# Pair attention: the softmax sum's reciprocal goes through memory and is applied to the aggregate; the weights are multiplied and stored in halves

## The chip, the cores and the metric

The kernel runs on one core of a Trainium2 chip. A time is the device time of one execution in microseconds. The kernel before took 7536.76 us, the median of three runs (7522.86 to 7555.75). The profile is of one further execution, recorded by the hardware profiler.

The core has five instruction streams that matter here[...]: TensorE (PE in the profile), VectorE (DVE), ScalarE (ACT), GpSimd (POOL) and SyncE (SP). They wait for each other by semaphores. SP and ACT also issue the DMA transfers of this stage. A DMA issue is an instruction in its engine's stream[...].

## The reference, cut to what matters

The program is a chain of eight layers on an activation `x` of shape (4, 64, 64, 128): deformable convolution, expert choice, triangle, recurrent, Fourier, mixture of experts, pair attention, mixture of experts. The change touches pair attention alone. For each of the four batch elements, with 64 rows, 64 columns, four heads and 32 channels per head, it computes:

```
p = (einsum('bxyi,ie->bxye', x, W) + b).reshape(B, N, N, HEADS, HD)
pn = layernorm(p, ln_g, ln_b)
scores = einsum('bxahd,bayhd->bxayh', pn, pn) / sqrt(HD)
att = softmax(scores, axis=2)
x_upd = layernorm(einsum('bxahd,bayhd->bxayhd', p, p), ln_g, ln_b)
agg = einsum('bxayh,bxayhd->bxyhd', att, x_upd).reshape(B, N, N, EMBED)
out = concatenate([x, agg], -1) @ Wf + bf
return layernorm(out, ln2_g, ln2_b)
```

The softmax runs over `a`. Its denominator, called z here, depends on head, x and y alone, and so does not depend on the index over which the aggregate sums. Dividing every weight by z before the sum over `a`, and dividing the finished sum by z, give the same result.

## The kernel before, in words

The four batch elements are computed one after another (the loop `for b in range(4)` at the end of `stage_pair_attention`). Each goes through three phases. The instructions of each engine are put in order when the program is built, by a list scheduler that uses its own estimates of time; the order in the source is not always the order that an engine runs.

**project** normalises x, projects it to p, and writes two copies to memory: `xd` (the normalised x, transposed) and `pd` (p by position). It keeps p, its squares and its normalised form in SBUF as `pT`, `p2` and `pn`.

**weights** computes for each head `rs`, the reciprocal standard deviation of the products p times p, and then the softmax. The heads go in two pairs, `hp` = 0 and 1, and i = 0 and 1 is the head within the pair. A tile `s[i]` of one head has 128 partitions (two values of `a`, times the 64 of x) and 2048 columns (two more values of `a`, the group index g from 0 to 15, and 64 columns y). `a` is 4 g plus two bits. The steps for one pair are:

- 128 small matmuls (line 2387) write the scores to PSUM tiles `po`; ACT copies them to `s` (L2413) and DVE keeps a running maximum (L2415).
- DVE reduces the maximum (L2420), PE swaps the two partition halves by a matmul (L2422), and DVE takes the larger (L2423).
- For each i, DVE subtracts the maximum (L2425) and ACT takes the exponential (L2426).
- For each i, four matmuls (L2430) sum the exponentials over partition halves and part of the columns into a PSUM tile `pz`. DVE then multiplies `s[i]` by `rs` in place (L2431), reduces `pz` to z (L2432), takes the reciprocal (L2433), and multiplies `s[i]` by it in place (L2434).
- Two DMAs per head (L2436), both on SP, write `s[i]` to the memory tensor `wd`, one for each half of the partitions. `wd` has the order head, a bits, x, g, y. Each contiguous piece is 1024 values, 4 KB.

The in-place product at L2431 overwrites what the matmuls of L2430 read, so that it can't start until the four matmuls of its head are done.

**combine** sums over `a`. The 64 rows x are done in eight blocks of 8 (`xg`), and each block has 64 units: 16 groups g times four heads. A unit is one matmul with 32 rows (`spread`, L2484), `S` from a tile `L` (p, loaded from `pd`) and a tile `R` (the weights, loaded from `wd`). DVE multiplies S by `q4` into `t` (L2496), for three or four units at once, and a second matmul per unit (`gather`, L2512) sums `t` into the PSUM accumulator `acc`. There are two S tiles, of four and three units, each with one buffer. `load_right` (L2461) fills one R for half of the groups of a block: `load_right(0)` reads g = 0 to 7 of the first block, `load_right(1)` reads g = 8 to 15. Each is eight DMAs, four on SP and four on ACT, and R is used only when all eight have landed. The first two loads are issued at the start of combine, and wait for the stores to `wd`.

At the end of each block `project_out` copies the accumulator from PSUM to `agg` (L2518, on ACT), does eight matmuls with the output weights (L2523 and L2524, into `pof`, which takes the one buffer that `acc` had), copies the result (L2526, ACT), adds the bias (L2527, POOL), and normalises it: statistics on DVE (L2531, L2532), a square root on ACT (L2534), a reciprocal and a small product on DVE (L2535, L2537), and scale and shift on ACT (L2539) and POOL. The tile `lx` (L2511), a load of `xd` on SP into the two buffers of the tag `xT`, is the other half of the concatenation.

Below, a "block end" is this passage from one accumulator to the next, with its 8 matmuls on PE.

Of the kernel before, what the change touches and what calls it, by code (L numbers as in the profile page):

```python
# [10 lines left out]
F32 = mybir.dt.float32  # L11
I32 = mybir.dt.int32
AF = mybir.ActivationFunctionType
ALU = mybir.AluOpType
AX = mybir.AxisListType
# [2201 lines left out]
def stage_pair_attention(k, w, bvec, ln_g, ln_b, wf, bf, ln2_g, ln2_b, blk32):  # L2217
# [14 lines left out]

    nc, tc = k.nc, k.tc
    with ExitStack() as octx:
        wp = octx.enter_context(tc.tile_pool(name="pa_w", bufs=1))
        dr = octx.enter_context(tc.tile_pool(name="pa_d", bufs=2, space=DRAM))
# [28 lines left out]
        both = wp.tile([128, 128], F32, tag="both", name="both")  # L2267
# [20 lines left out]
        sm = octx.enter_context(tc.tile_pool(name="pa_s", bufs=2))  # L2288
# [80 lines left out]
                nc.gpsimd.tensor_scalar(pn[:, c8, :], pn[:, c8, :], vec[:, 2:3], None, op0=ALU.add)  # L2369
            return pT, pn, p2  # L2370

        def weights(ps, wd, pT, pn, p2):
            rs = [big.tile([128, 2, 16, 64], F32, tag="rs", name="rs", bufs=4) for _ in range(4)]
            turn = [0]

            def products(hp, src):

                for a1 in range(2):
                    for half in range(2):
                        po = [ps.tile([128, 8, 64], F32, tag=t, name="po") for t in (("h0", "h1"), ("A", "B"))[turn[0] % 2]]  # L2380
                        turn[0] += 1
                        for j in range(8):
                            for i in range(2):
                                hr = slice(64 * hp + 32 * i, 64 * hp + 32 * i + 32)
                                for a2 in range(2):
                                    a = 4 * (8 * half + j) + 2 * a2 + a1
                                    nc.tensor.matmul(  # L2387
                                        po[i][64 * a2 : 64 * a2 + 64, j, :], src[hr, :, a], src[hr, a, :], start=True, stop=True
                                    )
                        at = (slice(None), a1, slice(8 * half, 8 * half + 8))  # L2390
                        for i in range(2):
                            yield i, at, po[i]

            for hp in range(2):
                for i, at, po in products(hp, pT):
                    nc.scalar.activation(rs[2 * hp + i][at], po, AF.Square, scale=1.0 / 32.0)
                for i, at, po in products(hp, p2):
                    t = rs[2 * hp + i][at]
                    nc.vector.tensor_tensor(t, po, t, op=ALU.subtract)
                    nc.gpsimd.tensor_scalar(t, t, 0.0, None, op0=ALU.max)  # L2400
            for r in rs:
                nc.scalar.activation(r, r, AF.Ln, bias=k.eps5)
            for r in rs:
                nc.scalar.activation(r, r, AF.Exp, scale=-0.5)
            R = [sixteen("X0", [8, 8, 64], "R0")]
            nc.gpsimd.memset(R[0], 0.0)
            for hp in range(2):
                pair = sixteen(("X3", "X2")[hp], [2, 2, 16, 64], "s")
                s = [pair[:, i] for i in range(2)]
                run = [sm.tile([128, 512], F32, tag="sq", name="run") for _ in range(2)]  # L2410
                wide = lambda t: t.rearrange("p (v y) -> p v y", y=64)
                for n, (i, at, po) in enumerate(products(hp, pn)):
                    nc.scalar.copy(s[i][at], po)  # L2413
                    if n >= 2:
                        nc.vector.tensor_tensor(wide(run[i]), po, wide(run[i]) if n >= 4 else s[i][:, 0, 0:8], op=ALU.max)  # L2415
                flat = lambda t: t.rearrange("p u v y -> p (u v) y")
                mx = sm.tile([128, 2, 64], F32, tag="mx", name="mx")
                z = sm.tile([128, 2, 64], F32, tag="z", name="z")
                for i in range(2):
                    nc.vector.tensor_reduce(mx[:, i, :], run[i].rearrange("p (v y) -> p y v", y=64), axis=AX.X, op=ALU.max)  # L2420
                    pm = ps.tile([128, 64], F32, tag="AB"[i], name="pmx")
                    nc.tensor.matmul(pm, swap, mx[:, i, :], start=True, stop=True)  # L2422
                    nc.vector.tensor_tensor(mx[:, i, :], mx[:, i, :], pm, op=ALU.max)  # L2423
                for i in range(2):
                    nc.vector.tensor_tensor(flat(s[i]), flat(s[i]), mx[:, i : i + 1, :].to_broadcast([128, 32, 64]), op=ALU.subtract)  # L2425
                    nc.scalar.activation(s[i], s[i], AF.Exp, scale=1.0 / math.sqrt(32.0))  # L2426
                for i in range(2):
                    pz = ps.tile([128, 8, 64], F32, tag=f"h{i}", name="pz")
                    for n in range(4):
                        nc.tensor.matmul(pz, both, flat(s[i])[:, 8 * n : 8 * n + 8, :], start=(n == 0), stop=(n == 3))  # L2430
                    nc.vector.tensor_tensor(s[i], s[i], rs[2 * hp + i], op=ALU.mult)  # L2431
                    nc.vector.tensor_reduce(z[:, i, :], pz.rearrange("p v y -> p y v"), axis=AX.X, op=ALU.add)  # L2432
                    nc.vector.reciprocal(z[:, i, :], z[:, i, :])  # L2433
                    nc.vector.tensor_tensor(flat(s[i]), flat(s[i]), z[:, i : i + 1, :].to_broadcast([128, 32, 64]), op=ALU.mult)  # L2434
                    for a2 in range(2):
                        nc.sync.dma_start(  # L2436
                            wd[2 * hp + i, 2 * a2 : 2 * a2 + 2].rearrange("a x g y -> x a (g y)"),
                            s[i][64 * a2 : 64 * a2 + 64].rearrange("p u v y -> p u (v y)"),
                        )
            R.append(sixteen("X1", [8, 8, 64], "R1"))  # L2440
            nc.gpsimd.memset(R[1], 0.0)
            return R

        def load_left(n, pd):
            xg, half = divmod(n, 2)
            for h in range(4):
                for a4 in range(4):
                    r = 32 * h + 8 * a4
                    (nc.sync, nc.scalar)[a4 % 2].dma_start(
                        Ls[n % 2][r : r + 8, :, 32 * a4 : 32 * a4 + 32],  # L2450
                        bass.AP(pd.tensor, pd.offset + (512 * xg + 32 * half + a4) * 128 + 32 * h, [[8192, 8], [512, 8], [1, 32]]),
                    )

        def combine(b, xd, pd, wd, Rs):
            with tc.tile_pool(name="pa_cp", bufs=1, space=PSUM) as ps:

                def load_right(n):
# [9 lines left out]
                groups, u = [], 0  # L2467
                while u < 512:
                    c = min((4, 3)[len(groups) % 2], 512 - u)
                    groups.append((u, c))  # L2470
                    u += c
                acc, out, lxs = {}, {}, {}

                def spread(i):
                    u0, c = groups[i]
# [26 lines left out]
                def gather(i):  # L2502
                    u0, c = groups[i]
                    t = out.pop(i)
                    for j in range(c):
                        xg, u = divmod(u0 + j, 64)
                        h = u % 4
                        if u == 0:
                            acc[0] = ps.tile([128, 512], F32, tag="acc", name="acc")
                            lx = lxs[xg] = sm.tile([128, 512], F32, tag="xT", name="lx")  # L2510
                            nc.sync.dma_start(lx, xd[:, 512 * xg : 512 * xg + 512])  # L2511
                        nc.tensor.matmul(acc[0][32 * h : 32 * h + 32, :], sum4, t[:, j, :], start=(u < 4), stop=(u >= 60))  # L2512
                        if u == 63:
                            project_out(xg)

                def project_out(xg):
                    agg = sm.tile([128, 512], F32, tag="sq", name="agg")
                    nc.scalar.copy(agg, acc[0])  # L2518
                    lx = lxs.pop(xg)
                    po = ps.tile([128, 4, 128], F32, tag="acc", name="pof")  # L2520
                    for j in range(4):
# [26 lines left out]
                for i in range(len(groups) + 2):  # L2548
                    if i < len(groups):
                        spread(i)  # L2550
                    if i >= 2:
                        gather(i - 2)

        ready = stats(0)
        for b in range(4):
            xd = dr.tile([128, 4096], F32, tag="xd", name="xd")
            pd = dr.tile([4096, 128], F32, tag="pd", name="pd")
            wd = dr.tile([4, 4, 64, 16, 64], F32, tag="wd", name="wd")
            with tc.tile_pool(name="pa_ps", bufs=2, space=PSUM) as ps:
                p = project(b, ps, xd, pd, *ready)  # L2560
                load_left(0, pd)
                load_left(1, pd)
                Rs = weights(ps, wd, *p)
            if b < 3:
                ready = stats(b + 1)
            combine(b, xd, pd, wd, Rs)


def prep_conv3(w):
# [57 lines left out]
```

## Time and profile before

| what | value |
|---|---|
| median of three runs | 7536.76 us |
| the profiled execution | 7520.84 us, its span 7519.0 us |
| TensorE / VectorE / ScalarE / GpSimd busy | 86% / 64% / 38% / 20% of the span |
| mean granted TensorE clock | 0.9 |
| pair attention in the trace | from about 5106 us to about 7176 us |
| combine, first S matmul to the last accumulator's copy, batch element 0 | 5283.21 to 5623.97 us |
| the same, elements 1, 2, 3 | 5798.47 to 6138.85, 6310.73 to 6650.49, 6822.56 to 7163.61 us |

Times are read from the start of the span. A row of a group gives line, engine, operation, output and inputs, the shape, and the number of instructions; after the first bar the busy time in us and the mean of one in ns; after the second the idle time of the engine before these instructions and what ended most of it. A row of the timeline has start, length, engine, line, operation, and in brackets the idle time before it with what ended it. "x8" on PE counts the records of the profile, of which a matmul on f32 has two. The chain of work is followed back from the end of a stretch, at each step to what released it. A row of the windows view has the busy time of PE, its weight loads, DVE, ACT and POOL, then the granted clock, the busy share of the 16 DMA engines, and the GB/s that they moved.

### The profile page before, as it was taken

The numbers are of one execution on the slowest core, as the hardware profiler recorded it, in microseconds if no ns is written. First come the engines' busy times: TensorE is split into PE (matmuls) and PEld (weight loads), VectorE is DVE, ScalarE is ACT, GpSimd is POOL, SyncE is SP. The second block draws the span as 40 slices with busy tenths as digits, with TensorE's granted clock in tenths as the row PEclk, the third lists the DMA queues.
The fourth block names the chain that finished last, engine by engine and source line by source line (L and its number), as shares of the span: only waits on it lengthen the run. The fifth ranks groups of instructions, "written<-read, shape, count | busy, mean of one in ns | idle before, by whom it ended". The sixth has DMA issues, their size and how long they took to land. (4 is left out here: it accounts for less than half of the span.)

```text
span 7519.0 us, 156903 instructions
## 1 busy us (share of the span) xinstructions
PE 6475.0 (86%) x63791; PEld 3490.8 (46%) x63791; DVE 4812.9 (64%) x10774; ACT 2842.8 (38%) x6717; POOL 1518.8 (20%) x1218
## 2 busy tenths in 40 slices
PE   7996888866688789799989988798897997998989
PEld 3443666654455553255555555445224234252244
DVE  2113877754577437588756566674885876857877
ACT  3332555543243326411156665564013022040055
POOL 0001222210011100055522221253012111120135
PEclk9997888987889899899989899797997997988989
DMA  4436788871300130300000000001111111111101
GB/s 120 98 89 195 210 246 242 244 227 60 137 1 2 34 67 9 116 23 23 25 10 9 9 10 4 9 1 42 34 25 50 26 39 34 27 32 41 23 23 31
DMA packets 673783, 498.10 MB, mean 66 GB/s; under 512 B 296822, under 2 KB 588600, under 8 KB 669208
## 3 DMA queue, kind: packets, MB, share of 16 engines
q1 hardware_dynamic: 510158, 399.80, 18.9%
q10 hardware_dynamic: 162890, 88.11, 4.4%
q8 instruction: 509, 8.34, 0.5%
q14 instruction: 226, 1.85, 0.1%
HBM read 335.28 MB, written 152.33 MB: 65 GB/s over the span
## 5 line engine op out<-in xcount | busy, mean ns | idle before, releaser
L2496 DVE TENSOR_TENSOR t<-S,q 128x1536 f32<-128x1536 f32 (+3 forms) x608 | 1157.0, 1949 | 120.7 <-PE S L2484 115.5
L2484 PE MATMUL S<-R,L 32*128 32x512 f32 x4096 | 734.6, 651 | 90.1 <-DMA R<-wd 78.6
L2512 PE MATMUL acc<-t,sum 128*32 128x512 f32 x4096 | 639.6, 608 | 0.0
L2198 PE MATMUL pe<-ew,yT 128*128 128x512 f32 x1024 | 480.6, 604 | 25.2 <-DVE xs L2204 22.3
L1797 PE MATMUL acc<-w,attT 128*64 128x264 f32 x4096 | 485.2, 390 | 11.0 <-DVE w L1793 11.0
L2484 PEld LDWEIGHTS S<-R,L 32*128 32x128 f32 x4096 | 200.4, 186 | 611.2 <-issue 280.1
L2518 ACT COPY agg<-acc 128x512 f32<-128x512 f32 x32 | 18.8, 586 | 1192.6 <-DMA L<-pd 855.4
L792 DVE COPY_PREDICATED band<-bit,band 128x384 f32<-128x384 int32 (+11 forms) x384 | 312.5, 929 | 186.4 <-ACT band L783 149.8
L773 PE MATMUL S<-kpad,qm 32*64 32x192 f32 (+3 forms) x8192 | 365.8, 405 | 72.4 <-ACT band L783 37.7
L2204 DVE SCALAR_TENSOR_TENSOR xs<-pe,gate,xs 128x128 f32<-128x128 f32 x1024 | 333.1, 346 | 96.9 <-PE pe L2198 80.3
L1790 POOL TENSOR_TENSOR w<-xtl,ei 128x528 f32<-128x528 f32 x256 | 332.1, 1319 | 310.5 <-ACT ei L1789 202.5
L1793 DVE TENSOR_TENSOR w<-xtl,pe 128x1056 f32<-128x1056 f32 x256 | 320.4, 1251 | 99.5 <-ACT ei L1789 88.6
L1797 PEld LDWEIGHTS acc<-w,attT 128*64 128x64 f32 x4096 | 283.5, 137 | 197.1 <-DVE w L1794 38.3
L2207 ACT ACTIVATE sc<-pe,gate 128x128 f32<-128x128 f32 x1024 | 291.2, 375 | 199.5 <-PE pe L2198 192.4
L773 PEld LDWEIGHTS S<-kpad,qm 32*64 32x64 f32 x8192 | 265.6, 151 | 128.8 <-issue 65.3
L514 PE MATMUL dw<-pad,diag 32*32 32x512 f32 x6912 | 307.4, 612 | 13.2 <-issue 7.3
L884 PE MATMUL pt<-ident,D 128*128 128x128 f32 x1536 | 259.8, 319 | 66.3 <-DMA D<-dd 48.4
L2512 PEld LDWEIGHTS acc<-t,sum 128*32 128x32 f32 x4096 | 92.7, 108 | 458.4 <-issue 436.1
L2198 PEld LDWEIGHTS pe<-ew,yT 128*128 128x128 f32 x1024 | 185.6, 193 | 232.1 <-issue 151.5
L2527 POOL TENSOR_TENSOR o<-o,bf 128x512 f32<-128x512 f32 x32 | 40.7, 1271 | 1228.5 <-ACT o L2526 1228.5
L886 ACT COPY dt<-pt 128x512 f32<-128x512 f32 x384 | 205.5, 595 | 146.2 <-PE pt L884 145.7
L884 PEld LDWEIGHTS pt<-ident,D 128*128 128x128 f32 x1536 | 214.6, 203 | 87.6 <-DMA D<-dd 52.3
(520 smaller groups left out, 12716.7 us busy)
## 6 DMA issues: line engine op xcount, KB each, us to landing
vb<-vd SPq DMA_DIRECT2D x272, 256.0 KB
D<-dd SPq DMA_DIRECT2D x128, 192.0 KB
D<-dd SPq DMA_DIRECT2D x128, 168.0 KB
D<-dd SPq DMA_DIRECT2D x128, 144.0 KB
w<-in_e_weight_dram ACTq DMA_DIRECT2D x16, 1024.0 KB
w<-in_e_weight_dram SPq DMA_DIRECT2D x16, 1024.0 KB
wd<-s SPq DMA_DIRECT2D x32, 512.0 KB
D<-dd SPq DMA_DIRECT2D x128, 120.0 KB
```

Of the source, the lines that this page charges most:

```text
L514: nc.tensor.matmul(acc[g][32 * c : 32 * c + 32], diag[r, j, tap, :], pads[j][r, y0 : y0 + 8, tx : tx + 64], start=(tap == 0), stop=(tap == 8),
L773: ins = nc.tensor.matmul(acc[g][64 * h : 64 * h + 64].rearrange("p (a s) c -> p a s c", a=3), qm[rows, h, m, :], keys, start=(m == 0), sto ...
L792: nc.vector.copy_predicated(flat[:, :, 0:n], bit[:, 0, :, i : i + 1].to_broadcast([128, 48, n]), flat[:, :, s : s + n])
L884: ins = nc.tensor.transpose(pt[:, g, :], D[:, g, ty : ty + 382 : 3], k.ident)
L1790: nc.gpsimd.tensor_tensor(w2[:, 2:4], xt[:, 2:4, 0:2], window(ei, 0, [[0, 2], [0, 2], [1, 132]]), op=ALU.mult)
L1793: nc.vector.tensor_tensor(w1, xt[:, :, 1:3], window(pe, 0, [[0, 4], [0, 2], [1, 132]]), op=ALU.mult)
L1797: nc.tensor.matmul(acc[b // 2][64 * (b % 2) : 64 * (b % 2) + 64], attT[:, b // 2, hp, 64 * (b % 2) : 64 * (b % 2) + 64], src[:, b].rearran ...
L2198: nc.tensor.matmul(pe[h].rearrange("p e c -> p (e c)"), yT[:, 128 * t : 128 * t + 128], ew[:, 4 * h : 4 * h + 4, :].rearrange("p e c -> p ...
L2204: nc.vector.scalar_tensor_tensor(xt, pe[0][:, e, :], gate[:, t, e : e + 1], xt, op0=ALU.mult, op1=ALU.add)
L2484: nc.tensor.matmul(S[:, j, :], Ls[n % 2][r, ag, :], Rs[n % 2][r, ag].rearrange("p x y -> p (x y)"), start=True, stop=True)
L2496: nc.vector.tensor_tensor(t[:, j0:j1].rearrange("p u (x y) -> p u x y", x=8), S[:, j0:j1].rearrange("p u (x y) -> p u x y", x=8), qf[:, q0 ...
L2512: nc.tensor.matmul(acc[0][32 * h : 32 * h + 32, :], sum4, t[:, j, :], start=(u < 4), stop=(u >= 60))
```

## The change

1. In `weights`, the product of the weights with 1/z (L2434) is dropped. z and its reciprocal are still computed, and for each head a [64, 64] tile is written to a new memory tensor `zd` by a DMA on SP: four per batch element.
2. Both heads' matmuls for z now stand before both heads' products with `rs`. The product of one head is split by g into two halves of 1024 columns. After each half, its two stores go out, one on SP and one on ACT: 16 stores of 256 KB per batch element instead of eight of 512 KB on SP alone. The contiguous pieces are 512 values, 2 KB.
3. In `combine`, `agg` is no longer copied by ACT: DVE multiplies the accumulator in PSUM by `zx`, a tile that a DMA on SP loads from `zd` for each block, every row of a head repeated for its 32 channels. `zx` takes a buffer of the tag `xT`, so that `lx` and `zx` of one block now hold both.

```diff
-        def weights(ps, wd, pT, pn, p2):
+        def weights(ps, wd, zd, pT, pn, p2):
...
+                pzs = []
                 for i in range(2):
-                    pz = ps.tile([128, 8, 64], F32, tag=f"h{i}", name="pz")
+                    pzs.append(ps.tile([128, 8, 64], F32, tag=f"h{i}", name="pz"))
                     for n in range(4):
-                        nc.tensor.matmul(pz, both, flat(s[i])[:, 8 * n : 8 * n + 8, :], start=(n == 0), stop=(n == 3))
-                    nc.vector.tensor_tensor(s[i], s[i], rs[2 * hp + i], op=ALU.mult)
-                    nc.vector.tensor_reduce(z[:, i, :], pz.rearrange("p v y -> p y v"), axis=AX.X, op=ALU.add)
+                        nc.tensor.matmul(pzs[i], both, flat(s[i])[:, 8 * n : 8 * n + 8, :], start=(n == 0), stop=(n == 3))
+
+                for g in range(2):
+                    c8 = slice(8 * g, 8 * g + 8)
+                    for i in range(2):
+                        nc.vector.tensor_tensor(s[i][:, :, c8], s[i][:, :, c8], rs[2 * hp + i][:, :, c8], op=ALU.mult)
+                        for a2 in range(2):
+                            (nc.sync, nc.scalar)[a2].dma_start(
+                                wd[2 * hp + i, 2 * a2 : 2 * a2 + 2, :, c8].rearrange("a x g y -> x a (g y)"),
+                                s[i][64 * a2 : 64 * a2 + 64, :, c8].rearrange("p u v y -> p u (v y)"),
+                            )
+                for i in range(2):
+                    nc.vector.tensor_reduce(z[:, i, :], pzs[i].rearrange("p v y -> p y v"), axis=AX.X, op=ALU.add)
                     nc.vector.reciprocal(z[:, i, :], z[:, i, :])
-                    nc.vector.tensor_tensor(flat(s[i]), flat(s[i]), z[:, i : i + 1, :].to_broadcast([128, 32, 64]), op=ALU.mult)
-                    for a2 in range(2):
-                        nc.sync.dma_start(
-                            wd[2 * hp + i, 2 * a2 : 2 * a2 + 2].rearrange("a x g y -> x a (g y)"),
-                            s[i][64 * a2 : 64 * a2 + 64].rearrange("p u v y -> p u (v y)"),
-                        )
+                    nc.sync.dma_start(zd[2 * hp + i], z[0:64, i, :])
...
-                acc, out, lxs = {}, {}, {}
+                acc, out, lxs, zxs = {}, {}, {}, {}
...
                             nc.sync.dma_start(lx, xd[:, 512 * xg : 512 * xg + 512])
+                            zx = zxs[xg] = sm.tile([128, 512], F32, tag="xT", name="zx")
+                            nc.sync.dma_start(zx, bass.AP(zd.tensor, zd.offset + 512 * xg, [[4096, 4], [0, 32], [1, 512]]))
...
                     agg = sm.tile([128, 512], F32, tag="sq", name="agg")
-                    nc.scalar.copy(agg, acc[0])
+                    nc.vector.tensor_tensor(agg, acc[0], zxs.pop(xg), op=ALU.mult)
...
+            zd = dr.tile([4, 64, 64], F32, tag="zd", name="zd")
```

More of the change, by code (lines that the diff above doesn't have):

```diff
@@ L2452, in load_left, with combine @@
                     )
-        def combine(b, xd, pd, wd, Rs):
+        def combine(b, xd, pd, wd, zd, Rs):
             with tc.tile_pool(name="pa_cp", bufs=1, space=PSUM) as ps:
@@ L2562, in stage_pair_attention @@
                 load_left(1, pd)
-                Rs = weights(ps, wd, *p)
+                Rs = weights(ps, wd, zd, *p)
             if b < 3:
                 ready = stats(b + 1)
-            combine(b, xd, pd, wd, Rs)
+            combine(b, xd, pd, wd, zd, Rs)
 def prep_conv3(w):
```

## The prediction

> **What bounds the kernel now.** I read first which engine carries the stage (the groups by line), then the chain of waits where the change acts, then the DMA windows beside it, then the timeline of one block end. The groups:
>
> ```profile
> L2496 DVE TENSOR_TENSOR t<-S,q 128x1536 f32<-128x1536 f32 (+3 forms) x608 | 1157.0, 1949 | 120.7 <-PE S L2484 115.5
> L2484 PE MATMUL S<-R,L 32*128 32x512 f32 x4096 | 734.6, 651 | 90.1 <-DMA R<-wd 78.6
> ...
> L2518 ACT COPY agg<-acc 128x512 f32<-128x512 f32 x32 | 18.8, 586 | 1192.6 <-DMA L<-pd 855.4
> ```
>
> Combine lasts about 341 us per batch element and DVE and PE are both nearly full in it; ACT, which copies agg, is idle. PE stands still once per element, 78.6 us in 4 waits for R<-wd: the passage from weights to combine. The chain of waits through that passage, element 0:
>
> ```profile
> 5254.47 5.65 PE pz L2430 x8
> ...
> 5260.24 2.29 DVE s L2431
> ...
> 5263.67 2.29 DVE s L2431
> 5265.96 2.20 DVE s L2434
> ...
> 5269.39 2.30 DVE s L2434
> 5271.74 0.57 SPq L2436
> ...
> 5272.37 5.92 DMA wd<-s
> ...
> 5281.32 1.88 DMA R<-wd
> 5283.21 2.12 PE S L2484 x8
> ```
>
> From 5260.24 to 5283.21 the end is set by four whole-tile products on DVE, then the stores, then the loads. The last store is issued at 5272.37 and lands at 5278.3; the four issues of the first R on each queue take 2.8 us; their data another 1.9. The other elements have 11.5 us between the last product and the first S too. The windows view says what the stores wait for:
>
> ```profile
> 5268.00:5270.00 2.00, 0.00 (x0) 0.00 (x0) 1.93 (x4) 0.00 (x0) 0.00 (x0) 0.66 0.30 68
> 5270.00:5272.00 2.00, 0.00 (x0) 0.00 (x0) 1.68 (x1) 0.00 (x0) 0.00 (x0) 0.50 0.97 195
> 5272.00:5274.00 2.00, 0.00 (x0) 0.00 (x0) 0.00 (x0) 0.00 (x0) 0.00 (x0) 0.50 0.98 281
> 5274.00:5276.00 2.00, 0.00 (x0) 0.00 (x0) 0.00 (x0) 0.00 (x0) 0.00 (x0) 0.50 0.99 336
> ```
>
> The DMA engines are full: 2.1 MB in 7.8 us, 270 GB/s, starting 1.4 us after the first issue and signalled 0.9 us after the last byte. A block end (block 4, element 0):
>
> ```profile
> 5498.73 1.05 PE L2512 MATMUL acc<-t,sum 128*32 128x512 f32 x2
> ...
> 5499.70 1.12 PE L2484 MATMUL S<-R,L 32*128 32x512 f32 x2
> ...
> 5499.86 0.59 ACT L2518 COPY agg<-acc 128x512 f32<-128x512 f32 x1 [33.71 <-DMA L<-pd]
> ...
> 5504.86 0.49 DVE L2531 BATCH_NORM_STATS2 st<-o 128x6 f32<-128x128 f32 x2 [4.10 <-POOL o L2527]
> ...
> 5509.17 1.14 PE L2484 MATMUL S<-R,L 32*128 32x512 f32 x8 [0.22 <-DVE t L2496]
> ```
>
> PE needs about 1.0 us per change between S and acc, for one unit ("x2") as for four ("x8"); in mid-block four such stretches (4 and 3 units) take 4.12 us, DVE 3.96 of them. At the block end DVE idles about 4 us.
>
> [...]
>
> **Part 1: the last pair of heads, per element.** pz of head 0 is done at 5260.24 as before. The compiled order on DVE is now: both halves of head 0 (1.2 us each, to 5262.6), reduction and reciprocal (0.68 + 0.55, to 5263.8; pz of head 1 ended at 5263.6), both halves of head 1 (5265.0 and 5266.1), reduction and reciprocal to 5267.3. The final weights are ready at 5266.1 instead of 5271.7: the two dropped products (2 x 2.29) and one reduction that now comes later. The stores start at 5261.5, so data flows from 5262.9; 2.1 MB at 270 GB/s end at 5270.7, signalled 5271.6 instead of 5278.3. The compiled waits let the first R start after the g < 8 halves, but its last issues reuse the completion semaphores of the last halves and of zd, so the load still ends behind everything: SP issues two loads (1.2) after 5271.6, data 1.9: first S at 5274.7, 8.5 us earlier. Bounds: at the first pair's store rate (windows at 5758 to 5767: about 225 GB/s) 7.0; if DMA were no limit, last half at 5266.2 + 1.4 + 1.3 + 0.9 + 3.1 = 5272.9, 10.3. The pieces are now 2 KB; xd's stores have such rows, and windows of 1 us at 5117 and 5126 show 262 and 249 GB/s at shares of 0.70 and 0.89, so I take no loss.
>
> **Part 2: the first pair of heads.** In element 1, DVE goes from product (5748.54) through 1/z to the second pair's running maxima, and reaches the reduction L2420 at 5763.17. After: halves of head 0 to 5750.9, z to 5752.1, halves of head 1 to 5754.45, z to 5755.7. ACT now has four stores in its stream ahead of the copies (L2413) of the second pair: the fourth waits for 5754.45 and takes 0.6, so the copies end at 5756.2 (before 5755.4). PE's next scores wait for the second pz to be reduced at 5755.15 and take 2.5 us, the last ones come at 5759.1, the six maxima end at 5760.6. Gain 2.6 us; bounds 1.5 (issues of up to 1.8 us, as other ACT issues here show) and 3.5. zd's stores are 16 KB and wait for nothing that matters; without that cover they cost about 0.6 us on SP.
>
> **Part 3: block ends.** agg is now a DVE product of 0.69 us instead of an ACT copy of 0.59, and it stands behind the t before it. pof starts 0.7 to 1.5 us later. What pays for it is the compiled order: PE now does all of the next group's S before pof, DVE has a t to do in its former idle time, and acc units come in larger stretches. Replayed by hand with 1.0 per stretch, 2.0 for the eight matmuls, 0.6 copy, 1.3 POOL, 1.2 statistics, 0.7 root, reciprocal, product. Block 4, from its last acc (0): before, S resumes at 10.44 (5509.17). After: S 1.0 to 2.05; agg 2.05 (t ends) to 2.75; pof to 4.75; S to 5.85 (this t waits for the unit behind pof); acc of six units in two rounds to 7.75; S, acc to 9.85. Gain 0.6. Block 0: acc 1.0, S (fourth unit waits for t, 2.43) to 3.5, pof 5.55, S 6.6, acc 8.5, S 9.55, then acc; before 9.16. Loss 0.4. The eight together: +0.4, +0.4, +0.6, -0.4, -0.5, -0.3, +0.7, +0.1 = +1.0 us per element, less 1.0 once, where ACT's DMA issues delayed agg (5415.06): +3 in all. Bounds -4 and +16. zx and lx can only be loaded after the previous block end, but have 42 us; SP's next loads come 13 us later (5332.07 to 5345.69)[...].[...]
>
> **Sum.** 4 x (8.5 + 2.6) - 3 = 41 us less: span 7478 from 7519.0, the profiled execution 7480 from 7520.84. That execution stands 16 us below the median, so 7536.76 - 41 = 7495.
>
> **Rivals.** (a) The block ends cost what pof is late, 1.4 us in each, because DVE's freed time buys nothing where PE is full: 32 x 1.4 = 45 eats the 44 of parts 1 and 2: no change, 7538. For it: PE is full in mid-block; against: PE has fewer stretches. (b) Small packets: if a 2 KB packet took as long as a 4 KB one, the stores end at 5278.5 and part 1 gains 0.7: 4 x (0.7 + 2.6) - 3 = 10 us, 7527. Against: xd's rate. A half effect gives 7511. (c) Slower: DVE's t behind agg waits for the S unit behind pof (above: idle from 2.75 to 5.85), and if PE can't recover that 3.1 us in any block end, 32 x 3.1 - 44 = +55, 7592. It beats the gains from 1.4 us per block end, and passes 0.5% from 2.6. For it: pof's place in the PE order; against: the replay finds PE ahead afterwards in three of the ends.
>
> **Numbers.** 0.5% is 38 us, about what a measurement of this kernel can tell from no change. My case 0.65, (a) 0.15, (b) in some degree 0.13, (c) 0.07. My own case spans 7476 to 7518 by its bounds and sits near the 0.5% line (7499); three quarters of it lie below. Faster 0.5, same 0.43, slower 0.07. With the spread of the runs (16 us each way) and (b) inside: 7470 to 7532; my case alone 7474 to 7515.
>
> **What would show it.** The first S after weights about 11 us earlier per element and PE's wait for R<-wd at about 45 us instead of 78.6 (right), or stores that run past 5275 (b). DVE's idle time before L2531 below 84.1 us and combine at 340 to 343 us per element (right); 352 would be (a), 366 (c). What makes me wrong: acc stretches of six that take more than 2 us, or stores on two queues that hold ACT longer than 1.8 us each.

## The result, and the profile after

The changed kernel takes 7487.44 us (7485.25 to 7494.74) beside 7538.66 us (7522.86 to 7555.75) for the kernel before: 51 us less, ratio 0.9938 with a 95% interval of 0.9918 to 0.9957. Measured again beside the experiments it took 7487.4 against 7531.99 us, ratio 0.9942 (0.9929 to 0.9955). So the change makes the kernel about 0.6% faster (the two intervals together reach from 0.4 to 0.8%), and 7487 lies 8 us below the forecast of 7495 and inside its range.

The profiled execution took 7485.25 us (span 7483.5); that of before 7520.84 (7519.0). To see where the 35.5 us between these two spans come from, I cut each batch element of the stage at three marks that both traces have: the first copy of scores (L2413, L2414 after), the first S of combine, and the last agg.

| us, summed over the elements | before | after | difference | forecast |
|---|---|---|---|---|
| first scores to first S ("passage", four) | 268.59 | 213.89 | -54.7 | -44.4 |
| first S to last agg ("combine", four) | 1361.97 | 1362.19 | +0.2 | +3 |
| last agg to the next first scores ("projection", three) | 316.78 | 323.13 | +6.35 | 0 |

The rest of the span, most of it other stages of the program, was 12.5 us longer in the execution after; the change doesn't touch it, and over the fourteen profiles of this document it lies between 5571 and 5596 us, with that of the kernel before (5572) among the shortest. The gain is where it was forecast, in the passage, and larger; the projection lost some 2 us per element that nobody had on the list.

The groups of the page, after:

```profile
L2503 DVE TENSOR_TENSOR t<-S,q 128x1536 f32<-128x1536 f32 (+3 forms) x608 | 1157.6, 1948 | 114.4 <-PE S L2491 110.0
L2491 PE MATMUL S<-R,L 32*128 32x512 f32 x4096 | 726.6, 651 | 50.0 <-DMA R<-wd 38.2
```

and three groups of the same view, kept apart by shape and taken over the four combines alone, the first of them before:

```profile
L2531 DVE BATCH_NORM_STATS2 st<-o 128x6 f32<-128x128 f32 x128 | 30.5, 280 | 84.1 <-POOL o L2527 84.1
...
L2540 DVE BATCH_NORM_STATS2 st<-o 128x6 f32<-128x128 f32 x128 | 30.4, 280 | 49.2 <-POOL o L2536 49.2
L2527 DVE TENSOR_TENSOR agg<-acc,zx 128x512 f32<-128x512 f32 x32 | 21.8, 682 | 4.9 <-PE acc L2521 4.9
```

PE's wait for R<-wd is 38.2 us where it was 78.6: 10 us less in each element. The agg product takes 682 ns on DVE (the copy on ACT took 586), and DVE's idle time ahead of the statistics has fallen from 84.1 to 49.2 us.

The chain of waits through the passage of element 0, after:

```profile
5260.47 4.79 PE pz L2432 x6
...
5265.38 0.78 DVE s L2437
...
5266.52 1.22 DVE s L2437
5267.74 0.61 DVE z L2444
...
5268.84 1.18 DVE s L2437
...
5270.03 4.11 DMA wd<-s
...
5274.23 0.57 SPq L2468
...
5277.16 2.03 DMA R<-wd
5279.19 2.11 PE S L2491 x8
```

From the first product to the first S it is now 5265.38 to 5279.19, 13.8 us where before has 22.97. The two products with 1/sum are gone from the chain, and the stores begin after one half. The store in this chain, issued at 5270.03, is that of the second head's g < 8 half, the last one that the first R reads; it lands at 5274.15 and releases the first issues of R. The last stores of all, issued at 5271.17, land at 5275.47, just before the third of SP's four issues of R (5275.49; the fourth ends at 5277.0). Then come the data of the last load. DMA in windows of 2 us (last two columns: share of the 16 engines, GB/s):

```profile
5268.00:5270.00 2.00, 1.53 (x4) 0.38 (x2) 1.97 (x4) 0.00 (x0) 0.00 (x0) 1.00 0.98 237
5270.00:5272.00 2.00, 0.00 (x0) 0.00 (x0) 1.97 (x4) 0.00 (x0) 0.00 (x0) 1.00 1.02 345
5272.00:5274.00 2.00, 0.00 (x0) 0.00 (x0) 0.33 (x1) 0.00 (x0) 0.00 (x0) 1.00 0.98 304
```

The engines are full, as before. From the start of the first packet of these stores to the end of the last, the 2.1 MB take 7.2 to 7.4 us in the four elements, about 290 GB/s in pieces of 2 KB; the kernel before took 8.5 us, about 250 GB/s in pieces of 4 KB.

The end of block 4, element 0, after (the timeline; the bracket is the idle time before the group):

```profile
5494.29 1.04 PE L2521 MATMUL acc<-t,sum 128*32 128x512 f32 x2
5495.27 1.13 PE L2491 MATMUL S<-R,L 32*128 32x512 f32 x6
5496.24 0.68 DVE L2527 TENSOR_TENSOR agg<-acc,zx 128x512 f32<-128x512 f32 x1
5496.98 0.49 PE L2532 MATMUL pof<-wf,lx 128*128 128x128 f32 x2 [0.57 <-DVE agg L2527]
...
5500.01 1.91 PE L2521 MATMUL acc<-t,sum 128*32 128x512 f32 x12
5500.12 2.29 DVE L2503 TENSOR_TENSOR t<-S,q 128x2048 f32<-128x2048 f32 x1 [3.19 <-PE S L2491]
```

agg waits for the t ahead of it, pof waits 0.57 us for agg, and then DVE stands 3.19 us because its next t needs the S unit that is queued behind pof. That is word for word the mechanism of rival (c); what it costs is the question of the later experiments.

### The profile page after: what moved, and what is told of

Same layout as the page of the kernel before. It is cut to its first block, busy times and chain, and to the rows that moved or that the text cites. A ratio compares the mean times of both kernels' runs of the same rounds, so it can differ in the third digit from the quotient of the medians.

```text
span 7483.5 us, 156976 instructions
## 1 busy us (share of the span) xinstructions
PE 6465.5 (86%) x63791; PEld 3490.3 (47%) x63791; DVE 4798.9 (64%) x10806; ACT 2822.3 (38%) x6685; POOL 1520.4 (20%) x1218
## 5 line engine op out<-in xcount | busy, mean ns | idle before, releaser
L2491 PE MATMUL S<-R,L 32*128 32x512 f32 x4096 | 726.6, 651 | 50.0 <-DMA R<-wd 38.2
L2535 ACT COPY o<-pof 128x512 f32<-128x512 f32 x32 | 18.8, 586 | 1257.8 <-DMA lx<-xd 857.2
L514 PE MATMUL dw<-pad,diag 32*32 32x512 f32 x6912 | 307.8, 614 | 12.5 <-issue 6.7
```

The costliest lines, as they stand in the source:

```text
L514: nc.tensor.matmul(acc[g][32 * c : 32 * c + 32], diag[r, j, tap, :], pads[j][r, y0 : y0 + 8, tx : tx + 64], start=(tap == 0), stop=(tap == 8),
L2491: nc.tensor.matmul(S[:, j, :], Ls[n % 2][r, ag, :], Rs[n % 2][r, ag].rearrange("p x y -> p (x y)"), start=True, stop=True)
```

## The experiments

All are edits of the changed kernel; a median stands beside the ratio to the kernel before of the same chip. Of the profile of each run I give the marks of the table above, per element; "product to first S" runs from the first product with rs of the last head pair to the first S. The runs stood on four chips, on which the kernel before has medians of 7532 to 7536 us, and the changed kernel was run again on the first of them alone; a difference between runs of two chips carries some 4 us from that.

### The changed kernel again, and its parts one at a time

> The changed kernel once more, beside the kernel before and the partial versions. 7487 us, 51 less than before (ratio 0.991 to 0.996); from the first product of the last head pair to the first S 13.7 us (before 22.95), combine 340.5 us per element.

Measured: 7487.4 us, ratio 0.9942 (0.9929 to 0.9955); passage 53.7, product to first S 13.7, combine 340.6 us.

**Only the 1/sum moved, products and stores whole.**

```diff
-                for g in range(2):
...
+                for i in range(2):
+                    nc.vector.tensor_tensor(s[i], s[i], rs[2 * hp + i], op=ALU.mult)
+                    for a2 in range(2):
+                        nc.sync.dma_start(
+                            wd[2 * hp + i, 2 * a2 : 2 * a2 + 2].rearrange("a x g y -> x a (g y)"),
+                            s[i][64 * a2 : 64 * a2 + 64].rearrange("p u v y -> p u (v y)"),
+                        )
```

> The 1/sum goes to zd and is applied to agg as in the changed kernel, but the weights are multiplied and stored whole, all on SP, as before. My theory, that both halves of the change matter: the two dropped products leave four 512 KB stores that start earlier and run at the 260 GB/s of the kernel before; from the first product to the first S 17.7 us per element (before 22.95, after 13.7), the first head pair gains about 2.7; 4 x (5.3 + 2.7) = 32 less a little at block ends: 29 us less than before. Rival 1, the halves buy nothing: the whole 51 us. Rival 2, the DMA engines set the end and the products nothing: 0 to 8 us.

Measured: 7495.62 us, ratio 0.9952 (0.9937 to 0.9967), 36 less than before. Passage 32.7 us less in all, product to first S 17.4, combine 339.9. The dropped products alone give 60% of the gain in the passage. By the passage both rivals fall; the medians alone (36 and 45 us less than before on this chip, with intervals that overlap) would not tell this run from rival 1.

**Only the halves, 1/sum still multiplied on DVE**, in halves too; each half's stores follow it, on SP and ACT as in the changed kernel.

```diff
-                    nc.sync.dma_start(zd[2 * hp + i], z[0:64, i, :])
+                    for g in range(2):
+                        c8 = slice(8 * g, 8 * g + 8)
+                        nc.vector.tensor_tensor(
+                            s[i][:, :, c8], s[i][:, :, c8], z[:, i].unsqueeze(1).unsqueeze(1).to_broadcast([128, 2, 8, 64]), op=ALU.mult
+                        )
...
-                    nc.vector.tensor_tensor(agg, acc[0], zxs.pop(xg), op=ALU.mult)
+                    nc.scalar.copy(agg, acc[0])
```

> Only the halves: products and stores in halves on SP's and ACT's queues, both heads' sums before the products, but 1/sum is multiplied into the weights on DVE as before and nothing is applied to agg. My theory: the first half begins 0.87 us earlier, because it waits for three of the four sums instead of all, and the first store leaves half a product earlier; from the first half to the first S 20.6 us where before has 22.95, so 3.2 per element with the earlier start, and under 0.9 in the first head pair: 13 to 16 us less than before. Rival 1 of the run above, which gives the halves nothing: 0. Rival 3, that halves on two queues make most of the gain: 35 to 45 us less, first half to first S near 15.

Measured: 7510.2 us, ratio 0.9966 (0.9953 to 0.9979), 22 less than before. Passage 16.6 us less in all, close to the 13 to 16 of my theory, and not the 35 of rival 3. From first half to first S 19.5. The two parts of the change add up in the passage: 32.7 + 16.6 = 49.3 of 54.7. That the total fell by more than the passage lies in combine, 338.4 per element, to which the clock comes in below.

**All stores on one queue.**

```diff
-                            (nc.sync, nc.scalar)[a2].dma_start(
+                            nc.sync.dma_start(
```

> The changed kernel with all sixteen half stores on SP, none on ACT. My theory[...]: the last stores are issued 0.5 to 1.3 us later (14.2 to 15.0 us from first half to first S instead of 13.7), and the copies of the second head pair, which now stand behind no store on ACT, come up to 1 us earlier: within 4 us of the changed kernel, either way. Rival, that the stores ran faster (300 GB/s against 260 before) because two queues fed them: they fall back to 260, 15 us or more, 5 us more than the changed kernel at least.

Measured: 7492.44 us, ratio 0.9949 (0.9936 to 0.9961), in total no difference from the changed kernel. But product to first S is 16.0 us, 2.3 more, and outside what I expected. From the timeline of element 0, the windows, and the view of SP's issues of these stores (least, median and longest in ns, then the starts of the first and the last):

```profile
5259.61 7.49 SPq L2439 DMA_DIRECT2D wd<-s  x8
5261.82 2.30 DVE L2437 TENSOR_TENSOR s<-s,rs 128x1024 f32<-128x1024 f32 x2
...
5262.00:5264.00 2.00, 0.51 (x2) 0.00 (x0) 2.00 (x2) 0.00 (x0) 0.00 (x0) 1.00 0.85 280
5264.00:5266.00 2.00, 0.00 (x0) 0.00 (x0) 1.27 (x3) 0.00 (x0) 0.00 (x0) 1.00 0.83 196
...
L2439 SPq DMA_DIRECT2D wd<-s x8: 574/602/1030, 5259.6 to 5266.1; - x8
```

SP is at its eight issues for 7.49 us and ends 3 us after the last product. Six of them take the 0.6 us that I had reckoned with, the last two take 1.0 each, and ahead of the fourth SP waits 1.5 us for the second head's first product. So the last store is issued 7.7 us after the first product, where the changed kernel has 5.8, and has landed after 11.7 instead of 10.1. The engines are not full meanwhile (shares 0.85 and 0.83). So the second queue did save issue time here, and more of it than I allowed. The rival's mark, 15 us or more, was met too, but by stores that came late to engines that were partly idle; whether the second queue also brought bandwidth, this run can't tell. The expected gain in the first head pair did not come: 12.0 us from product to L2421 with ACT's four stores and without them, since the copies wait for PE there. Of the 8.8 us that the passage lost, 6.4 were given back by a combine of 338.3 in three elements, again the clock.

### What holds the first product

The chain shows the first product behind pz: it writes s in place, and pz reads s. rs's tile is free after the product, so it can take the result.

```diff
-                        nc.vector.tensor_tensor(s[i][:, :, c8], s[i][:, :, c8], rs[2 * hp + i][:, :, c8], op=ALU.mult)
+                        w = rs[2 * hp + i]
+                        nc.vector.tensor_tensor(w[:, :, c8], s[i][:, :, c8], w[:, :, c8], op=ALU.mult)
...
-                                s[i][64 * a2 : 64 * a2 + 64, :, c8].rearrange("p u v y -> p u (v y)"),
+                                w[64 * a2 : 64 * a2 + 64, :, c8].rearrange("p u v y -> p u (v y)"),
```

> The changed kernel, but the product of exponentials and rs is written into rs's tile (which nothing needs afterwards) and stored from there, so that it no longer waits for the sums pz, which read s. If the wait for pz is what sets the first product, it starts at the end of the exponentials, 4.5 us earlier, the stores then run back to back at about 300 GB/s and the first S comes 3 to 4.5 us earlier in each element; the first head pair gains 0 to 1.5, being bound by PE there: 12 to 24 us less than the changed kernel. If the DMA engines or pz set the end anyway (the reciprocals of pz stand on SP between the loads of R), less than 5 us.

Measured: 7462.91 us, ratio 0.9906 (0.989 to 0.9921), 24 us under the changed kernel, 16.5 of them in the passage and 3.9 in combine (by the clock, see below). The product comes 4.6 us earlier after the maxima (6.78 us instead of 11.4), the first S 4.1; the first head pair gains nothing. Then the first R, loaded as soon as what it reads is stored:

```diff
+                    if hp and not g:
+                        for x in range(8):
+                            ld = (nc.sync, nc.scalar)[x % 2].dma_start(
+                                R[0][x::8, :, x, :], bass.AP(wd.tensor, wd.offset + x * 1024, [[65536, 16], [64, 8], [1, 64]])
+                            )
...
-                load_right(0)
                 load_right(1)
```

The g >= 8 stores and the zd stores of this pair are ordered behind these loads on their queues.

> The run above, and in the second head pair the loads of the first R are issued between the stores of the g < 8 halves, which are all they read, and those of the others. The first S comes 1.5 to 2.5 us earlier than in the run above, 5 to 6.5 earlier than in the changed kernel: 22 to 35 us less than the changed kernel. If the loads compete with the stores or R1 comes too late for unit 32, the run is no faster than the one above.

Measured: 7448.42 us, ratio 0.9881 (0.986 to 0.9902), 39 us under the changed kernel. Product to first S falls from 14.2 to 12.2 us, passage to 47.4. The timeline of element 1 shows products that no longer wait for pz, and loads between the stores:

```profile
5758.59 9.19 PE L2432 MATMUL pz<-s,both 128*128 128x512 f32 x16 [3.77 <-ACT s L2427]
5758.91 4.62 DVE L2438 TENSOR_TENSOR rs<-s,rs 128x1024 f32<-128x1024 f32 x4
5766.39 2.49 SPq L2448 DMA_DIRECT2D R<-wd  x4
5768.98 1.29 SPq L2440 DMA_DIRECT2D wd<-rs  x2
```

Most of the gain beyond the passage's 6.1 us per element is in combine (337.3 in three elements), again by the clock.

### What the later agg costs

> The changed kernel with the product that makes agg done twice on DVE (0.68 us, the same values), so that pof starts 0.68 later in each of the 32 block ends. My theory, that DVE's idle time and the S units done ahead cover it: under 8 us more, combine 340.5 to 342.5 us per element. Rival a, that a block end costs what pof is late: 32 x 0.68 = 22 us more, combine 346.

```diff
+                    zx = zxs.pop(xg)
+                    for _ in range(2):
-                    nc.vector.tensor_tensor(agg, acc[0], zxs.pop(xg), op=ALU.mult)
+                        nc.vector.tensor_tensor(agg, acc[0], zx, op=ALU.mult)
```

Measured: 7511.28 us, ratio 0.9967 (0.9955 to 0.9979), 24 us over the changed kernel; combine 347.9. My theory falls. The run is not as clean as I meant it: in three ends of eight the compiled order puts the second product behind a whole t, so that pof comes 1.9 us later after the last acc, and the block that follows is 2.2, 2.4 and 1.1 us longer. In the four where the products stand together pof is 0.8 later and the block 0.79, 0.36, 0.38 and 0.16 longer, 0.42 on average. DVE's idle time ahead of the statistics doesn't cover a late pof: in these ends a fifth of it or more is passed on, half of it on average. Then the DVE product of the change ought to have cost something too. To see it I took it out, in two orders of PE. Both kernels leave the division by the sum out, so that what they compute differs; they only time the block ends.

```diff
-                    nc.vector.tensor_tensor(agg, acc[0], zxs.pop(xg), op=ALU.mult)
+                    nc.scalar.copy(agg, acc[0])
```

> The changed kernel with agg copied by ACT as before and no zx: the division by the sum is left out. Weights as in the changed kernel, block ends with the order of PE and DVE of the kernel before. The seven block ends between aggs took 293.2 us per element in the changed kernel and 294.2 to 294.7 in the kernel before; I expect 294.5 here, and a total within 6 us of the changed kernel. If moving agg to DVE had cost what pof is late (0.7 us or more a block end), this would be 20 us or more faster than the changed kernel.

Measured: 7477.81 us, ratio 0.9924 (0.991 to 0.9938); combine 340.3; the seven stretches from one agg to the next take 294.0 us per element, as in the kernel before (294.4). The total is 10 us under the changed kernel all the same; in the profile 8.4 of that lie in the projection. Then the same with the order of the changed kernel, by calling project_out later:

```diff
                         if u == 63:
-                            project_out(xg)
+                            held.append((xg, i, j + 1))
+                            return
...
                         spread(i)
+                    release()
```

(release calls project_out and then goes on with the gather that stopped.)

> The run above (division left out, ACT copies agg), but project_out is called after the next group's S, so that PE does three or four S units ahead of pof in every block end, as in the changed kernel, where the kernel before has one or two in five of eight. If that order is what paid for the later agg, the seven block ends take 287 to 291 us per element where the run above has 294.5: 14 to 30 us less in all. If the order is worth nothing and agg on DVE cost nothing, 294 again and no difference.

Measured: 7454.78 us, ratio 0.9899 (0.9885 to 0.9913), 23 us under the run before it; combine 334.3; the seven stretches 288.2. The groups of PE in these two runs, agg on ACT with the order of before:

```profile
L2491 PE MATMUL S<-R,L 32*128 32x512 f32 x4096 | 734.3, 651 | 49.6 <-DMA R<-wd 38.2 <-DVE t L2503 10.9
```

and with the order of the changed kernel:

```profile
L2491 PE MATMUL S<-R,L 32*128 32x512 f32 x4096 | 716.6, 651 | 44.3 <-DMA R<-wd 38.4 <-DVE t L2503 5.9
```

The same 4096 matmuls keep PE busy for 17.7 us less, because they come in fewer stretches, 152 of S per element instead of 156: a stretch of S takes about 1.1 us and one of acc about 1.05, for one unit as for four, and 16 stretches of S fewer make about 17.6 us. The kernel before has 156 of these stretches too, the changed kernel 152. So the change did two things in a block end that cancel: the order it brought is worth 6.1 us per element (combine 340.3 to 334.3), and the product on DVE costs 6.3 in nearly that order (334.3 to 340.6; three ends differ by one S unit ahead of pof). In that order the product makes pof start later after the last acc, by 5.0 us per element over the eight ends, so that here a late pof is passed on in full (the run with agg on ACT has no load of zx either).

### The clock at the start of combine

The seven stretches after the first agg are alike to 0.2 us in every run with the changed kernel's block ends (293.2 to 293.4); the first block, from the first S to the first agg, takes 47.3 us in the changed kernel and 45.1 in three elements of the run with stores on SP. The windows from the first S of element 1, after (PEclk is the third column from the end):

```profile
5780.76:5783.76 3.00, 3.00 (x14) 1.26 (x14) 0.85 (x1) 0.00 (x0) 0.00 (x0) 0.50 0.38 101
5783.76:5786.76 3.00, 2.30 (x11) 0.52 (x8) 3.00 (x2) 0.00 (x0) 0.00 (x0) 0.50 0.12 48
5786.76:5789.76 3.00, 3.00 (x15) 0.71 (x14) 2.40 (x2) 0.00 (x0) 0.00 (x0) 0.50 0.00 0
5789.76:5792.76 3.00, 3.00 (x24) 0.53 (x22) 1.76 (x1) 0.00 (x0) 0.00 (x0) 0.95 0.00 0
```

and before:

```profile
5798.47:5801.47 3.00, 3.00 (x14) 1.26 (x14) 0.86 (x1) 0.00 (x0) 0.00 (x0) 0.50 0.28 61
5804.47:5807.47 3.00, 3.00 (x15) 0.71 (x14) 2.39 (x2) 0.00 (x0) 0.00 (x0) 0.50 0.00 0
5807.47:5810.47 3.00, 3.00 (x20) 0.46 (x14) 1.76 (x1) 0.00 (x0) 0.00 (x0) 0.92 0.00 0
```

For 9 us from the first S on, PE's granted clock is 0.50. The kernel before does too: its clock is at 0.50 until 9.2 to 9.5 us after the first S of each element, that of the changed kernel until 9.1 to 9.5. So this stretch is no difference between the two, but it may cost both. To test it, PE is given something to do in the gap:

```diff
+            pw = ps.tile([128, 8, 64], F32, tag="h0", name="pw")
+            for n in range(6):
+                nc.tensor.matmul(pw, both, flat(s[1])[:, 8 * (n % 4) : 8 * (n % 4) + 8, :], start=True, stop=True)
```

> The changed kernel with six matmuls on the weights between the last product and the first S, whose result nobody reads. The traces show TensorE's granted clock at 0.50 for the first 4 to 9 us of combine after an idle stretch, and the first block of an element 2.2 us longer where it lasts 9. If that is the clock alone, the clock stays at 1.00, the first block takes 44 to 45.1 us instead of 47.3, and the kernel 9 to 13 us less. If the first block is long for another reason (the loads of R1 and L, buffers), nothing changes, or the six matmuls delay the first S.

Measured: 7484.31 us, ratio 0.9934 (0.9919 to 0.995), no difference, first block 47.3 again. In element 1 the clock stayed at 1.00 until 5782 and then fell all the same: six matmuls end 3.25 us before the first S. That settles nothing. With range(9) in the same place:

> The changed kernel with nine idle matmuls instead of six in the gap before the first S, so that PE stands still for about 1 us there instead of 3.5. If the clock falls because of the gap, it stays at 1.00 now, the first block of an element takes 43.5 to 45.1 us instead of 47.3 and the kernel 8 to 14 us less than the changed one. If the ninth matmul delays the first S, up to 1 us per element of it is lost. If the first block is long for another reason, it stays at 47.3.

Measured: 7467.89 us, ratio 0.9918 (0.9905 to 0.9931), 20 us under the changed kernel; combine 337.4, first block 44.1, first S not delayed; PE stands still for 0.74 us. Windows of element 1 from its first S:

```profile
5768.49:5771.49 3.00, 1.99 (x14) 0.77 (x14) 1.80 (x1) 0.00 (x0) 0.00 (x0) 1.00 0.36 92
5771.49:5774.49 3.00, 2.46 (x19) 0.78 (x22) 3.00 (x3) 0.00 (x0) 0.00 (x0) 1.00 0.15 57
```

The clock is the cause of the long first block: combine shows 12.7 us of it, 3.2 in each element. What the median gained beyond that, the profile has in stages that the edit doesn't touch.

### Everything together

> The whole computation, with what the runs before it gave: products written into rs, the first R between the halves' stores, three idle matmuls in the gap before the first S, and project_out called after the next group's S (agg stays a DVE product). With the first two alone the kernel took 7448 us. The matmuls close a gap of 3 us that left the clock at 1.00 in three of four elements already: 0 to 3 us less. The order of PE is that of the changed kernel in five of eight block ends and differs by one S unit in three: 0 to 2 us either way. So 7442 to 7450, combine 337.4 us per element. If the deferred call does more than the order shows, combine falls towards 334.

The edit is the two of "What holds the first product", the delayed call of project_out with agg as a DVE product, and three idle matmuls. Measured: 7430.63 us (7417.08 to 7448.71), ratio 0.9854 (0.9836 to 0.9872), the lowest median of all and below what I expected, though its interval overlaps that of the kernel with the first two edits (0.986 to 0.9902). Passage 47.5, combine 336.0: the first block takes 44.1 in every element, and after ends 4 to 6 (the first is end 0), where PE now does a fourth S unit ahead of pof so that DVE's next t need not wait behind it, the blocks are 0.42, 0.40 and 0.62 us shorter. That accounts for about 8 us against the kernel with the first two edits alone. The rest of the 18 between the medians no stage of the profile shows; the profiled execution was the slowest of the four, so it may be chance.

## Why the prediction was right, and where it was not

**Part 1** forecast 8.5 us per element from the first product to the first S; the trace has 9.25 (22.95 to 13.7). The path was right: in three of the four elements SP issues two of its four loads of R ahead of the last store's landing and two behind it, as the forecast had it. Its two terms were both off a little. The last store lands 10.1 us after the first product, where it had 11.4: the data took 7.3 us and not 7.8, and the landing was told 0.4 us after the last byte and not 0.9. From there to the first S it is 3.6 us where it had 3.1. That the second queue bought issue time is shown, by the 2.3 us that one queue costs; that it brought no bandwidth was my estimate and is not shown, since the engines were partly idle in that run, and whether the smaller pieces or the second queue raised the rate from 250 to 290 GB/s no run separates. The prices of DVE's products held: the half of 1024 columns, put at 1.2 us, took 1218 ns (the median of L2437 after), as a t of that width did before (1218, a form of L2496), where the whole product took 2293 (L2431 before).

**Part 2** forecast 2.6 and the trace has 2.7 (14.7 to 12.0). Its worry over ACT's four stores was idle: without them the time is the same.

**Missed in both:** the first half begins 0.87 us earlier. It overwrites columns that only three of the four pz matmuls have to have read by then. Two head pairs in four elements make 7 us, the larger part of what the passage gained beyond the forecast.

**Part 3** forecast +1 us per element for the block ends, and combine came out equal (+0.05). Its replay was right end by end. It counts from the last acc of a block; from last acc to last acc the ends 0 to 6 changed by +0.30, +0.25, +0.49, -0.62, -0.42, -0.36 and +0.52 us (means of four elements), where its list has +0.4, +0.4, +0.6, -0.4, -0.5, -0.3 and +0.7: every sign is right, and every size within 0.25; the seven add up to +0.2 where the list has +0.9. (For block 4 its text has a gain of 0.6 and its list 0.5.) Counted from agg to agg the same ends look different, the first block 1.2 us longer and the other seven stretches 1.1 shorter, because the first agg now starts 1.3 us after its last acc, where it followed within 0.2 before, and the last agg follows at once in both; from the first S to the last acc of the first block it is 46.0 us in both. What the replay did not do is size the two effects apart, which are some 6 us per element each. The load of zx took 2.7 us (the first in the trace, from first to last packet; from 5281.5 to 5283.5 the busy share of the 16 engines is 0.25 to 0.27, at 98 to 102 GB/s) and lands 4.6 to 5.3 us after its issue; the next loads of L and R are issued 11.9 us after it at the earliest.

Rival (a), that a block end costs what pof is late, has the cost about right: half of the delay was passed on, on average, in the clean ends with agg done twice, and all of it where the product on DVE is set against the copy on ACT in nearly one order. What it lacked is that the new order of PE pays it back. The order is not in what the change says; the built programs have it where agg stands on DVE and, unless project_out is called later, not where it stands on ACT. Rival (c)'s idle time of DVE is there, 3.19 us in ends 4 to 6, and changing the order in these three ends gave 0.4 to 0.6 us in each, not 3.1.

**Rival (b)** falls: the 2 KB pieces ran no slower (about 290 GB/s where the 4 KB pieces had 250).

**Not in the sum at all:** the clock in the projection. Windows of 4 us show a clock of 0.73 to 0.84 from 4 to 12 us after the last agg and of 0.72 to 0.86 from 52 to 60 us where the projection takes 107.1 us or more, and 1.00 at these places where it takes 104.5 to 105.1, from the same instructions; with the first of the two dips alone it takes 105.9 to 106.9. All 42 projections of the fourteen profiles fall into these three kinds. Before has one with both dips and two with none, after has three with both: +6.35 us. The changed kernel itself, run again, had 104.5, 107.9 and 107.4, so I count this as chance and not as a cost of the change; no run settles whether the change makes the slower kind likelier.

By the medians, the forecast of 41 us fell 10 short of the 51 measured, and the passage's gain was underrated by as much (54.7 for 44.4). The single pair of profiles shows 35.5 because the projection and the other stages, by chance as far as is known, ran 19 us longer in the one after.

## What to carry to other kernels

When a forecast rests on a new instruction in a full loop, compare the compiled order as well and cost the two apart: here they were worth +6.3 and -6.1 us per element and looked like nothing. Compare such times between marks that the change doesn't itself move: agg moved against acc, and made two stretches look changed that were not. Before shortening a chain of products and stores, look at what its first link waits for; writing the product into a dead tile, so that it need not wait for a reader of its own input, shortened the passage by another 16.5 us, where the change itself had gained 54.7. And a gap of TensorE ahead of a dense stretch cost twice here, once as the gap (about 9.6 us in each element of the changed kernel) and once by the clock at 0.50 after it (3.2 us), so idle matmuls in it can pay; they did with a gap of 0.6 to 1.1 us left, and did not with 3.1 to 3.7.

## What the runs showed of the hardware

- TensorE's granted clock was at 0.50 after a gap of 9.6 us (the changed kernel), stayed at 1.00 over one of 0.74 us, and between 3.1 and 3.7 us it went either way (lost at 3.13, 3.25, 3.30, 3.55 and 3.67, kept at 3.09, 3.13 and 3.59). It came back about 4 us after the first S in three elements of the run with stores on SP and 9.1 to 9.5 us after it in the changed kernel, with the same instructions. The stretch at 0.50 around the first S of an element is 23.9 us long in the kernel before and 13.65 in the changed one; no run shows what sets its length. What I had not expected is the size beside a small change: 12.7 us in combine (where, from the first S on, the clock is as long at 0.50 before the change) and 6 in the projection, where the change as a whole is worth 51.
- With all stores on one queue, six of eight issues of 256 KB stores took 0.57 to 0.61 us and the last two 1.0 each (element 0); the first eight issues of R's loads on SP in the changed kernel took 0.53 to 0.60 (element 0).
- An order of PE that groups S and acc units differently at the block ends changed the busy time of 4096 equal matmuls from 734.3 to 716.6 us, with 152 stretches of S per element instead of 156.
